# First attention: maxima in a bank of the transposed scores' ring, a step later, and values between a step's two kinds of scores

## The chip, the cores and the metric

The kernel runs on one core of one Trainium2 chip. The metric is the device time of one execution in microseconds (us). TensorE is called PE in the profile (its weight loads PEld), VectorE DVE, ScalarE ACT, GpSimd POOL, SyncE SP.

## The reference: a small latent attention, the first of four

The whole program is two attentions with a feed-forward block behind each, twice, over x of 2 x 512 x 512 in fp32: eight residual steps. The change lies in the first of them alone:

```python
C_q = x @ Wq_d + bq_d                      # 512 -> 12
C_kv = x @ Wkv_d + bkv_d                   # 512 -> 4
q = (C_q @ W_qk + b_qk).reshape(b, s, 32, 4)
scores = einsum('bqhd,bkd->bhqk', q, C_kv) / sqrt(4)
attn = softmax(scores, axis=-1)            # no mask: 512 x 512 per head
V = (C_kv @ Wv_u + bv_u).reshape(b, s, 32, 16)
out = einsum('bhqk,bkhd->bqhd', attn, V)
return out.reshape(b, s, 512) @ Wo + bo
```

There are 2 batches x 32 heads, and each head has a score matrix of 512 x 512. The keys are only four numbers wide, so the matmuls are small and the scores have to be reduced (for the maxima) and exponentiated in full.

## The kernel before

Each head's scores are computed twice. Once as they stand, queries on the partitions, only to find the maximum of each row: `score` (L586) makes one 128 x 512 block with a matmul over 32 rows of the array and reduces it on DVE (L597) to one column of `nm`. And once transposed, keys on the partitions, with the maximum already subtracted: `transposed` (L621) makes a block (L627) and ACT takes its exponential into `probs` (L630). The subtraction needs no extra operation, since the negative maxima stand in spare rows of the queries: `maxima` (L611) transposes `nm` with four matmuls (L615), adds the queries with a fifth (L616, recorded at L199), and ACT copies the result to `qm` (L618). `split` (L601), two small POOL operations, divides the maxima into a high and a low part before that. `values` (L632) multiplies four blocks of exponentials with the values; as fp32 it runs as eight matmuls of two passes.

Four heads form a quartet, one in each quarter of 32 rows of the array; matmuls in different quarters can run side by side. There are 16 quartets, u = 0 to 15 (`quartets`, L573). A quartet takes 8 steps. In each step the queue of PE receives

- `next_scores()`: two scores, of quarters 0, 1 in even steps and 2, 3 in odd ones. Scores run twelve steps ahead: those of quartet u+1 end with step 3 of quartet u, where `split` follows;
- two transposed blocks of quartet u;
- in even steps one call of `values` for a block of keys that was finished at least two steps earlier (the list `behind`);
- in odd steps a call of `slices` (L757): a piece of other work from the list `extra` (projections and head preparation of the second batch first, then division, output projection and the start of the feed-forward block); some pieces hold no matmul, and the piece `add` is a POOL operation alone. In the last quartet there are slices in every step, two in the odd ones;
- in step 6 `maxima(u + 1)`.

PE's order is that of the code here (`tc.manual_schedule(engines={PE})`), so what stands at the head of PE's queue and waits holds all that is behind it. The other engines get their instructions in an order that the framework plans.

PSUM has eight banks of 128 x 512. They are dealt out by hand (L578 to L584): scores take banks 0, 1, 2 in turn ("S"), transposed blocks 3, 4, 5 ("T"), `values` bank 6, slices bank 7. A matmul that writes a bank waits until the bank's last reader (DVE for S, ACT for T) is done. `maxima` takes its turn in the S ring. In the last quartet, when no scores are left, slices also use banks 0 to 2.

Of the kernel before, what the change touches and what calls it, by code (L numbers as in the profile page):

```python
# [38 lines left out]
B, S, D = 2, 512, 512  # L39
# [389 lines left out]
def attn_latent_small(k, a):  # L429
# [9 lines left out]
    with ExitStack() as ctx:  # L439
# [134 lines left out]
        last = len(quartets) - 1  # L574
# [7 lines left out]
        def own_bank(kind):  # L582
            turns[kind] = (turns[kind] + 1) % 3
            return k.held[:, banks[kind][turns[kind]]]  # L584
# [25 lines left out]

        def maxima(u):  # L611
            b, half, i = quartets[u]
            tp = own_bank("S")
            for qt in range(NT):
                nc.tensor.transpose(tp[:, bass.ts(qt, P)], nm[u % 2][:, qt], k.ident)  # L615
            k.correct(tp, unit, qs[b][:, 4 * half + i])  # L616
            t = lp.tile([P, S], F32R, tag="qm", name="qm")
            nc.scalar.copy(t, tp)  # L618
            qm[u] = t

        def transposed(u, kc, g):  # L621
            b, half, i = quartets[u]
            if (u, kc) not in probs:
                odd = kc % 2
                probs[u, kc] = lp.tile([P, 4, S], F32, tag="pT", name="pt") if odd else k.other()
            ps = own_bank("T")
            nc.tensor.matmul(  # L627
                ps, keys[b][rows[g], bass.ts(kc, P)], qm[u][rows[g]], start=True, stop=True
            )
            nc.scalar.activation(probs[u, kc][:, g], ps, AF.Exp)  # L630

        def values(u, kc):  # L632
            b, half, i = quartets[u]
            acc = k.held[:, of_values]
            pt = probs.pop((u, kc))
            for g in range(4):
                nc.tensor.matmul(  # L637
                    acc[rows[g]],
                    vals[b][:, kc, i],
                    pt[:, g],  # L640
                    start=(i == 0 and kc == 0),
                    stop=(i == 3 and kc == NT - 1),
                )
            if i == 3 and kc == NT - 1:
                raws[u] = one([P, S], "raw")
                nc.scalar.copy(raws[u], acc)
                extra.extend(following(u))
# [66 lines left out]
        def following(u):  # L714
            b, half, i = quartets[u]
            if half == 0:
                return [divide(u)]
            if b == 1:
                return [divide(u)] + tail() + [project(u)]
            bias = lambda: blocks[0].bias  # L720
            pairs = []
            for t in (0, 2):
                pairs += [centre(t, t + 1, bias=bias), adapt(t), adapt(t + 1), put(t), put(t + 1)]
            return (
                [divide(u), begin(), project(u)]
                + pairs
                + [keep()]
                + [product(0), product(1), centre(0, 1), product(2), product(3)]
                + [put(0, True), put(1, True), centre(2, 3)]
            )  # L730
# [8 lines left out]
        def next_scores():  # L739
            at = next(scores, None)  # L740
            if at:
                u, qt, p = at
                for g in (2 * p, 2 * p + 1):
                    score(u, qt, g)
                if (qt, p) == (NT - 1, 1):
                    split(u)

        def run(pieces):
            for piece in pieces:
                for _ in piece:  # L750
                    pass

        def fill(n, bank):
            for _ in range(n):
                nc.tensor.matmul(k.held[:, bank], unit, keys[0], start=True, stop=True)

        def slices(cost):  # L757

            if not extra:
                fill(3, k.ring[-1])  # L760
            with tc.issue_after(first):
                while extra and cost > 0:
                    done = next(extra[0], None)
                    if done is None:
                        extra.pop(0)
                    else:
                        cost -= done

        k.ring = k.EVERY
        with tc.manual_schedule(engines={mybir.EngineType.PE, mybir.EngineType.DVE}):  # L770
            k.warm(30)
            for t in range(0, NT, 2):
                pair = [k.statistics(t + i) for i in range(2)]
# [28 lines left out]
        behind = []  # L802
        with tc.manual_schedule(engines={mybir.EngineType.PE}):
            for n in range(12):
                next_scores()
                slices(1)
                fill(2, of_values)
                if n == 7:
                    with tc.issue_after(k.latest):
                        adapter_coefficients(k, a)  # L810
                if n == 8:
                    maxima(0)
            run(extra)
            extra = later
            k.ring = other
            for u in range(len(quartets)):
                if u == last:
                    k.ring = (0, 1, 2, 7)
                for step in range(8):
                    next_scores()  # L820
                    for g in (2, 3) if step % 2 == 0 else (0, 1):
                        transposed(u, step // 2, g)
                    if step == 6 and u < last:
                        maxima(u + 1)
                    if step % 2 == 0 and len(behind) > 1:
                        values(*behind.pop(0))
                        if u == last:
                            slices(1)
                    else:
                        slices(2 if u == last else 1)  # L830
                    if step % 2:
                        behind.append((u, step // 2))
            k.ring = (0, 1, 2, 3, 4, 5, 7)
            for at in behind:
                values(*at)
            run(extra)
# [4 lines left out]
def adapter_coefficients(k, a):  # L841

    nc = k.nc
    k.coef = k.const.tile([P, 1], F32, tag="coef", name="coef")
    starts = k.load_row(a["f0_starts"], 4, "f0_starts", dtype=I32)
    rows = k.load(a["c_lora"], [P, 4], "c_lora", 1)
    startf = k.sm(4, "startf", 1)
    nc.vector.tensor_copy(startf, starts)


    c = k.sm(4, "le", 1)
    nc.vector.tensor_scalar(c, startf, rows[:, 3:4], None, ALU.is_le)
    r = k.sm(3, "rank", 1)
    both = k.sm(2, "adapter", 1)
    nc.vector.tensor_tensor(both, c[:, 1:3], c[:, 2:4], ALU.mult)
    nc.vector.tensor_tensor(r[:, 0:2], c[:, 1:3], both, ALU.subtract)
    nc.vector.tensor_copy(r[:, 2:3], both[:, 1:2])
    nc.vector.tensor_tensor(r, r, rows[:, 0:3], ALU.mult)
    nc.vector.tensor_reduce(k.coef, r, AX.X, ALU.add)
# [1292 lines left out]
@with_exitstack  # L2152
def kernel(ctx: ExitStack, tc: tile.TileContext, a: dict, out: bass.AP):
    k = Block(ctx, tc, a["x"], out)
    k.hold()
    block = attn_latent_small(k, a)
    bound = CausalBound(k, a)
    attn_gqa(k, a, bound, block)
    ffn_lora(k, a, block)
    attn_mla(k, a)  # L2160
    k.release(ctx)
    with k.tc.tile_pool(name="f1", bufs=2) as own:
        experts = Experts(k, a, own)
        with k.tc.tile_pool(name="heads", bufs=1) as pool:
            rooms = HeadRooms(k, a, pool)
            experts.first(rooms.fill)
            attn_mha(k, a, bound.register(), rooms, experts)
        experts.end()
# [168 lines left out]
```

## Time and profile before

| | us |
|---|---|
| median of 3 runs | 1975.5 (1972.48 to 1975.85) |
| the profiled execution | 1973.68 |
| its span, first to last instruction | 1971.9 |
| in it: the sixteen quartets | about 42 to 254 |
| PE busy in the span | 1928.5 (98%) |
| DVE busy | 1372.9 (70%) |
| ACT busy | 932.6 (47%) |
| POOL busy | 1024.6 (52%) |
| in 233 to 254, where no scores are left: DVE busy | 6.62 of 21 |
| one reduction of scores (L597), median | 0.680 |
| one exponential (L630), median | 0.597 |

The clock of PE is full (0.998 granted). Busy shares are means over stages with different limits; what matters for this change is the order of rows between 42 and 254 us. A matmul's row is longer than the time until the next may start, because matmuls are pipelined: distances are read from start to start. Two matmuls of one line that follow each other at once are merged into one row of the timeline ("x2"). The maxima of quartets 1 to 15 are transposed at 51.91, 64.57, 76.46, 88.97, 101.08, 114.58, 126.46, 138.33, 151.04, 164.10, 180.05, 193.80, 208.34, 220.64 and 233.56 us (starts of the first L615 row of each); they mark the quartets in the timeline.

### The profile page before, as it was taken

How to read it: one execution, taken by the hardware profiler on the slowest of the kernel's cores; microseconds unless marked ns; L12 is line 12 of the kernel's file. 1: busy time of each engine (PE TensorE's matmuls, PEld its weight loads, DVE VectorE, ACT ScalarE, POOL GpSimd, SP SyncE). 2: the span in 40 equal slices, each digit the busy share in tenths (PEclk: the TensorE clock that was granted, in tenths of full speed). 3: DMA queues.
4: the chain of work that ended last, by engine and by line, in shares of the span. 5: the costliest groups of instructions: out<-in, count | busy, mean ns of one | idle time of the engine just before them, and what ended most of it. 6: DMA issues, size and time to landing. Idle time of an engine off the chain costs nothing.

```text
span 1971.9 us, 40474 instructions
## 1 busy us (share of the span) xinstructions
PE 1928.5 (98%) x15608; PEld 1193.8 (61%) x15608; DVE 1372.9 (70%) x3456; ACT 932.6 (47%) x2450; POOL 1024.6 (52%) x1122
## 2 busy tenths in 40 slices
PE   9989999999999999999999999999999999999998
PEld 5333356777777777777776545666566544654654
DVE  8889658767776676777775576777677755847843
ACT  3876624444444443544443266666666311641640
POOL 4331055776756667677764256565656445216211
PEclk9999999999999999999999999999999999999999
DMA  4010222322321322232223213020101002002001
GB/s 136 17 44 1 76 68 70 87 77 89 93 71 40 97 76 81 76 97 76 78 79 84 71 22 109 7 73 7 62 13 55 28 6 48 2 2 44 1 2 43
DMA packets 69152, 108.96 MB, mean 55 GB/s; under 512 B 13906, under 2 KB 48722, under 8 KB 61908
## 3 DMA queue, kind: packets, MB, share of 16 engines
q1 hardware_dynamic: 68660, 104.15, 18.0%
q8 instruction: 127, 2.08, 0.5%
q0 software_dynamic: 288, 2.10, 0.3%
q14 instruction: 77, 0.63, 0.1%
HBM read 80.00 MB, written 4.19 MB: 43 GB/s over the span
## 4 chain that ended last, share of the span: by engine, by line
PE 87%; DVE 5%; POOL 4%; issue 1%; ACT 1%; DMA 0%; SPq 0%; DVEq 0%; ACTq 0%; POOLq 0%
PE held L1004 13%; PE held L281 11%; PE held L1139 9%; PE held L190 8%; PE held L357 8%; PE held L637 3%; PE held L589 3%; PE held L1076 3%; PE sc L190 2%; PE held L473 2%; PE tp L190 2%; PE held L1498 2%; PE held L1495 2%; PE pj L190 1%; PE held L1496 1%
## 5 line engine op out<-in xcount | busy, mean ns | idle before, releaser
L302 ACT ACTIVATE room<-room,nmax 128x128 f32<-128x128 f32 (+3 forms) x384 | 212.6, 557 | 354.9 <-DVE nmax L292 352.4
L281 PE MATMUL held<-kT,q 128*32 128x32 f32 (+15 forms) x4096 | 264.0, 397 | 6.2 <-DVE invs L310 2.3
L292 DVE CUSTOM_DVE_ANT_0 room<-held,mask 128x128 f32<-128x128 f32 (+3 forms) x384 | 178.9, 487 | 63.7 <-PE held L281 58.2
L281 PEld LDWEIGHTS held<-kT,q 128*32 128x32 f32 x4096 | 143.5, 110 | 87.4 <-issue 35.8
L357 PE MATMUL held<-turned,vals 32*128 32x384 f32 (+7 forms) x2784 | 189.5, 416 | 1.2 <-issue 1.2
L597 DVE TENSOR_REDUCE nm<-held 128x1 f32<-128x512 f32 x256 | 161.5, 682 | 23.5 <-PE held L627 13.9
L357 PEld LDWEIGHTS held<-turned,vals 32*128 32x128 f32 (+1 forms) x2784 | 149.3, 167 | 40.1 <-issue 23.5
L315 ACT ACTIVATE room<-room,invs 128x128 f32<-128x128 f32 (+3 forms) x312 | 151.3, 551 | 41.0 <-DVE invs L310 40.9
L254 DVE TENSOR_TENSOR rows<-rows,held 128x512 f32<-128x512 f32 x198 | 129.4, 673 | 31.9 <-PE held L1004 31.4
L330 DVE STREAM_TRANSPOSE turned<-room 128x1152 f32<-128x1152 f32 x80 | 107.9, 1361 | 40.7 <-ACT room L315 21.6
L243 POOL TENSOR_TENSOR rstd<-ve,mhalf 128x1 f32<-128x1 f32 x64 | 36.2, 569 | 177.1 <-DVE ve L241 177.1
L1165 POOL TENSOR_TENSOR q<-q,room 128x256 f32<-128x256 f32 x64 | 45.2, 727 | 123.6 <-DVE q L1148 113.0
L1183 POOL TENSOR_TENSOR q<-q,cosq 128x512 f32<-128x512 f32 x60 | 88.0, 1467 | 31.5 <-DVE t L1180 31.5
L1139 PE MATMUL held<-room,w 128*128 128x256 f32 x384 | 95.0, 383 | 0.0
L1184 POOL TENSOR_TENSOR q<-q,t 128x512 f32<-128x512 f32 x64 | 86.7, 1355 | 6.3 <-DVE q L1183 2.5
L302 ACT ACTIVATE probs<-probs,nmax 128x128 f32<-128x128 f32 (+3 forms) x128 | 70.7, 553 | 40.6 <-DVE nmax L292 39.8
L589 PEld LDWEIGHTS held<-keys,qs 32*128 32x128 f32 x256 | 30.9, 181 | 94.2 <-DVE nm L597 68.1
L1004 PE MATMUL held<-w,ctxT 128*128 128x256 f32 x360 | 86.5, 383 | 0.1
L630 ACT ACTIVATE pt<-held 128x512 f32<-128x512 f32 x128 | 69.7, 599 | 30.0 <-PE held L627 25.7
L589 PE MATMUL held<-keys,qs 32*128 32x512 f32 x256 | 77.1, 494 | 5.4 <-DVE nm L597 5.1
L630 ACT ACTIVATE room<-held 128x512 f32<-128x512 f32 x128 | 69.7, 599 | 26.7 <-PE held L627 23.2
L1519 POOL TENSOR_TENSOR q<-t,t 64x512 f32<-64x512 f32 x62 | 78.9, 1272 | 4.9
(435 smaller groups left out, 4949.4 us busy)
## 6 DMA issues: line engine op xcount, KB each, us to landing
w<-in_b_wq SPq DMA_DIRECT2D x16, 1024.0 KB, 4.9
w<-in_b_wo SPq DMA_DIRECT2D x16, 1024.0 KB, 4.9
vals<-v SPq DMA_DIRECT2D x256, 64.0 KB, 2.1
w<-in_m_wo SPq DMA_DIRECT2D x8, 1024.0 KB, 6.7
w<-in_b_wk SPq DMA_DIRECT2D x16, 256.0 KB, 2.8
w<-in_b_wupv SPq DMA_DIRECT2D x16, 256.0 KB, 2.6
w<-in_m_wqn SPq DMA_DIRECT2D x8, 384.0 KB, 3.5
rows<-in_x SPq DMA_DIRECT2D x8, 256.0 KB, 4.6
```

The source lines that it names most:

```text
L190: last = self.nc.tensor.matmul(out, lhsT, rhs, start=(i == 0), stop=(i == len(pairs) - 1))
L254: self.nc.vector.tensor_tensor(x, x, ps.rearrange("p (t d) -> p t d", t=2), op)
L281: nc.tensor.matmul(ps[32 * i : 32 * i + 32, a - lo : b - lo], q[:, at : at + 32], keys[:, a:b], start=True, stop=True,)
L292: nc.vector.tensor_tensor_reduce(out=row, in0=ps[:, :kv], in1=self.mask_back[:, :kv] if qt % 2 else self.mask[:, S - kv :], op0=ALU.add, o ...
L302: nc.scalar.activation(row, row, AF.Exp, bias=nmax, scale=-1.0, accum_out=total[:, qt : qt + 1])
L315: self.nc.scalar.activation(row, row, AF.Identity, scale=each)
L357: self.nc.tensor.matmul(out[:, :, :n], values(i, j), rhs, start=(j == blocks[0]), stop=(j == stop[i]),)
L589: nc.tensor.matmul(ps, qs[b][rows[g], 4 * half + i, bass.ts(qt, P)], keys[b][rows[g]], start=True, stop=True,)
L597: k.latest = nc.vector.tensor_reduce(nm[u % 2][:, qt, at : at + 1], ps, AX.X, ALU.max, negate=True).ins
L630: nc.scalar.activation(probs[u, kc][:, g], ps, AF.Exp)
L1004: k.nc.tensor.matmul(out, lhsT[:, i, bass.ts(t, P)], rhs[i], start=not (after or t or i), stop=i == 1, skip_group_check=True,)
L1139: nc.tensor.matmul(out, lhsT[:, c], rhs[:, c], start=c == 0, stop=c == 1)
```

## The change

Three things, all in the loop over quartets and in `maxima`:

- `maxima` takes its bank from the T ring.
- `maxima(u + 1)` moves from step 6, behind the transposed blocks, to step 7, between the scores and the transposed blocks.
- In a step, `values` (or the slice) comes between the scores and the transposed blocks, and no longer behind them; only the slice of step 7, and the additional slice of the last quartet's even steps, stay behind. The pairs of quarters change places: transposed blocks take quarters 0, 1 in even steps and 2, 3 in odd ones. Step 7 of the last quartet has one slice where it had two.

```diff
         def maxima(u):
             b, half, i = quartets[u]
-            tp = own_bank("S")
+            tp = own_bank("T")
...
                 for step in range(8):
                     next_scores()
-                    for g in (2, 3) if step % 2 == 0 else (0, 1):
+                    if step == 7 and u < last:
+                        maxima(u + 1)
+                    pair = (2, 3) if step % 2 else (0, 1)
+                    held = step % 2 == 0 and len(behind) > 1
+                    if held:
+                        values(*behind.pop(0))
+                    elif step < 7:
+                        slices(2 if u == last else 1)
+                    for g in pair:
                         transposed(u, step // 2, g)
-                    if step == 6 and u < last:
-                        maxima(u + 1)
-                    if step % 2 == 0 and len(behind) > 1:
-                        values(*behind.pop(0))
-                        if u == last:
-                            slices(1)
-                    else:
-                        slices(2 if u == last else 1)
+                    if step == 7 or held and u == last:
+                        slices(1)
                     if step % 2:
                         behind.append((u, step // 2))
```

## Prediction

> **What bounds the kernel now.** I read the page first, then the list of waits between 50 and 245 us (the stretch of this attention's sixteen quartets), then the timeline there, one engine at a time. Below, S is the pair of score matmuls of a step (L589), T its pair of transposed-score matmuls (L627), V one block of values (L637), X a slice of other work, M the four transposes and the correction for the maxima (L615, L199).
>
> ```profile
> PE 1928.5 (98%) x15608; PEld 1193.8 (61%) x15608; DVE 1372.9 (70%) x3456; ACT 932.6 (47%) x2450; POOL 1024.6 (52%) x1122
> ```
>
> ```profile
> PEld held L589 <- DVE nm L597: 61.4, 90, 1.0
> ```
>
> TensorE is busy throughout, and after the attention nothing stands still for long: what this stretch gains or loses, the end gains or loses. Inside the stretch the longest wait is that of S for a reduction on DVE. Whether that wait costs anything is seen in the timeline. Columns are start, length, engine, line. First PE with a full slice (two fp32 matmuls, L473) in each odd step:
>
> ```profile
> 85.58 0.50 PE L589 MATMUL held<-keys,qs 32*128 32x512 f32 x2
> 85.58 0.49 PE L627 MATMUL held<-qm,keys 32*128 32x512 f32 x2
> 86.01 1.07 PE L637 MATMUL held<-room,vals 128*32 128x512 f32 x8
> 87.00 0.50 PE L589 MATMUL held<-keys,qs 32*128 32x512 f32 x2
> 87.01 0.50 PE L627 MATMUL held<-qm,keys 32*128 32x512 f32 x2
> 87.44 1.13 PE L473 MATMUL held<-w,wv_diag 128*128 128x512 f32 x2
> 88.50 0.50 PE L589 MATMUL held<-keys,qs 32*128 32x512 f32 x2
> ```
>
> S and T start together: they use different quarters of the array's rows, so four matmuls take one pass. From start to start a pass takes 0.43 us, V 1.00, X 1.06, so two steps take 0.43+1.00+0.43+1.06 = 2.92 us with no gap: PE sets the pace. Then PE, DVE and ACT where the slices hold no matmul:
>
> ```profile
> 124.49 0.50 PE L589 MATMUL held<-keys,qs 32*128 32x512 f32 x2
> 124.50 0.50 PE L627 MATMUL held<-qm,keys 32*128 32x512 f32 x2
> 124.86 0.50 PE L589 MATMUL held<-keys,qs 32*128 32x512 f32 x1
> 125.77 0.50 PE L589 MATMUL held<-keys,qs 32*128 32x512 f32 x1 [0.42 <-DVE nm L597]
> 125.77 0.50 PE L627 MATMUL held<-qm,keys 32*128 32x512 f32 x2
> 126.46 0.63 PE L615 MATMUL held<-ident,nm 128*128 128x128 f32 x4 [0.19 <-DVE nm L597]
> 126.84 0.48 PE L199 MATMUL held<-qs,unit 128*128 128x512 f32 x1
> 127.25 1.06 PE L637 MATMUL held<-pt,vals 128*32 128x512 f32 x8
> 128.25 0.50 PE L589 MATMUL held<-keys,qs 32*128 32x512 f32 x2
> ```
>
> ```profile
> 125.02 2.48 DVE L597 TENSOR_REDUCE nm<-held 128x1 f32<-128x512 f32 x4 [0.22 <-PE held L627]
> 128.78 1.89 DVE L597 TENSOR_REDUCE nm<-held 128x1 f32<-128x512 f32 x3 [1.27 <-PE held L627]
> ```
>
> ```profile
> 125.09 1.08 ACT L630 ACTIVATE room<-held 128x512 f32<-128x512 f32 x2 [0.37 <-PE held L627]
> ```
>
> Here a loop sets the pace: S at 124.49, its reduction starts at 125.02 and takes 0.69, the second S of the next step needs that bank and starts at 125.77 (1.28 after the first S), V comes 0.43 later and S again 1.00 after V: 1.28+0.43+1.00 = 2.71 us for two steps. M costs more than its own 0.8 us here: it takes a bank of the S ring, waits for a reduction (126.46 in place of 126.20), and DVE then idles 1.27 us, because S of step 7 stands behind M and V.
>
> **The change, part by part.** It adds and removes no instruction, transfer or element; it reorders PE's queue and gives M a bank of the T ring. SP's and POOL's queues keep their order (the two small POOL operations that split the maxima are issued at step 3 as before, now four steps ahead of M).
>
> *Values or slice between S and T.* Before the queue reads [S T] V [S T] X. After it reads S V [T S] X [T S] V: a T pair now shares its pass with the next step's S pair. The pairs (0,1) and (2,3) are swapped, so the two pairs of a pass still use four different quarters. Within a quartet the number of passes stays, so a PE-paced pair of steps stays at 2.92. In the DVE-paced stretch the second T of a step now stands in front of S and waits for the bank of the T three back: T at 124.50, exponent at 125.09, done 0.60 later, hence 1.19, and about 0.05 to hand over (125.71 to 125.77 on the DVE side): 1.24, against 1.28 for the wait of S that is there anyway. I take 2.71 as unchanged, by 0.04 us of cover; without that cover every such pair of steps is longer by what ACT is late. On ACT itself the two exponents of a step need 1.08 us; four of them and a copy of a head fit 2.71, just.
>
> *The ends of the quartet.* At step 7 the queue becomes [T6 S7] M T7 X, and at step 0 of the next quartet S0 V [T0 S1]. X now lies between T7 and S0, so each has a pass to itself: nine passes in a quartet in place of eight. A pass with a single pair takes as long as one with two, as the end of the stretch shows, where no scores are left:
>
> ```profile
> 230.22 0.50 PE L627 MATMUL held<-qm,keys 32*128 32x512 f32 x2
> 230.65 1.06 PE L637 MATMUL held<-room,vals 128*32 128x512 f32 x8
> ```
>
> So +0.43 per quartet where PE sets the pace; where it doesn't, nothing (lower end zero).
> [...] I hold to the row: the whole pass is paid.
>
> *M in the T ring.* M no longer waits for DVE (its bank's exponent was issued before V and is done), which takes away 0.25 us at about half the quartets and 0.04 elsewhere. But it takes one of three banks: T7's first matmul needs the bank of T6's first (exponent done 1.19 after T6), its second that of T6's second (0.59+1.08 = 1.67, with the hand-over 1.73). M ends at 0.43+0.81 = 1.24. So T7's second waits 0.48, and X, S0 and V stand behind it. Nothing covers that where PE sets the pace.
>
> From the pass [T6 S7] to [T0 S1] the new order therefore takes 1.73 + 0.43 (T7) + X + 0.43 (S0) + 1.00 (V) = 3.59 + X; with no matmul in X, S0 shares T7's pass: 1.73+0.43+1.00 = 3.16. The two steps before it take the larger of 2.71 and 1.86+X. Against this stands the interval in the timeline of before, from S of step 5 to S of step 1 of the next quartet. By the time of M:
> - full slices. M at 52: 2.92+4.65 = 7.57 against 6.85 (49.79 to 56.64), +0.72. At 76 (the slice before M is four transposes, hence 2.71): +0.70. At 221: 7.57-6.67 = +0.90. At 180 and 194, with slices of 1.72: 3.58+5.31 = 8.89 against 8.03 and 8.18, +0.86 and +0.71. At 164 DVE has no gap (7.32): PE alone would give +0.25, a DVE that runs dry +0.9; I take +0.6. Together +4.5.
> - short slices (a head, 0.43, or four transposes, 0.59). At 65: 2.71+4.02 against 6.58, +0.15; at 89: 2.92+4.02-6.45 = +0.49; at 138 and 208: 2.71+4.18-6.46 = +0.43 each; at 151 (DVE with two more operations): +0.3. Together +1.8.
> - no matmul in the slice. At 115: 2.92+3.16-6.47 = -0.39; at 126: 2.71+3.16-6.46 = -0.59. Together -1.0.
> - at 101 the slice waits for POOL and DVE until 104.31 either way, and S0 and V follow as before: 0.
> - the ends: S0 of the first quartet alone +0.43; in the last but one T3 alone (no scores left) +0.43, and the wait of T7 +0.48. Together +1.3.
>
> Sum: 4.5+1.8-1.0+1.3 = +6.6 us. The last quartet holds the same pieces in the same number (eleven slices, twelve before with the last one empty): 0.
> The profiled execution took 1973.68 us, 1971.9 of it span and 1.8 around it: 1980.3 for it. It lies 1.8 under the median of the three runs, 1975.5; the middle of the four times is 1974.6, and 1974.6+6.6 is 1981, which I predict.
>
> **The rivals.**
> - *DVE sets the pace and gains (ends faster).* Freed of M, the S ring lets S7 go out one V and one M earlier, and the DVE gap of 1.27 us before 128.78 shrinks. Where that decides, a boundary gains 0.6 (the case at 126). For all fifteen that is -9; it needs eight of fifteen to break even with 0.7 lost at the others. For it: DVE has a gap of 0.6 to 1.4 us behind M at thirteen of the fifteen. Against it: at all but two (those at 115 and 126) the slice of step 7 puts a matmul and a pass of its own behind T7, and the rows around 86 show PE without a gap. With ten gaining, -6+3.5 = -2.5; at twelve -5: about 1969.
> - *The T wait takes the place of the S wait (slower still).* 0.04 us of cover is thin. If exponents come 0.2 late (the head copies share ACT, which is busy 10.0 of 11 us between 65 and 76), each of some 24 DVE-paced pairs of steps loses 0.2: +5 on top, 1986; at 0.5 it is +12, 1993.
> - *Nearly nothing.* If the single passes overlap their neighbours, the sum is 6.6-5.4 = about +1: 1976.
>
> **How the numbers follow.** Forecast (+4 to +10, 1978 to 1985 of its own): 0.56. Gain: 0.13. T wait: 0.14. Nearly nothing: 0.17. Slower by over 0.2% (3.95 us, about what a measurement of this kernel can tell from no change) are the forecast and the T wait: 0.70; within 0.2%: 0.17; faster: 0.13. The range of 8 in 10 takes in the nearly-nothing case with the scatter of the runs (1972.5 was seen) and the T wait at 0.2 and a little more: 1972 to 1988.
>
> **What would show it.** In the changed profile: M directly behind a pass [T S], with no wait for DVE; T of step 7 with its second matmul some 0.5 us late, released by an exponent (L627 waiting for L630, 4.6 us in six places before, more than 10 after); S of step 0 alone in a pass of 0.43 before V; 2.92 and 2.71 us per two steps unchanged in the middle of quartets; the quartet from M at 76 to M at 89, 12.5 us, near 13.4; that from 115 to 126, 11.9, near 11.3. I am wrong if the middle of the quartets changes its period, or if the second T of step 7 finds its bank free.

## The result and the profile after

| | before | after |
|---|---|---|
| median, us | 1975.5 (1972.48 to 1976.82, 5 runs) | 1982.67 (1981.73 to 1984.58, 5 runs) |
| ratio, 95% interval | | 1.0039 (1.0027 to 1.0050) |
| the profiled execution; its span | 1973.68; 1971.9 | 1983.25; 1981.5 |
| first M of all to the start of the last matmul of V | 218.14 | 225.42 (+7.28) |

The changed kernel is 0.39% slower, 7.2 us by the medians. Nearly all of it lies in the sixteen quartets: from the first maxima (37.1 and 37.5 us) to the last values block they take 7.28 us more.

The page shows nothing of this; PE's share does not move. Columns: engine, busy us (share) x instructions.

```profile
PE 1940.8 (98%) x15608; PEld 1201.5 (61%) x15608; DVE 1372.4 (69%) x3456; ACT 931.2 (47%) x2450; POOL 1025.8 (52%) x1122
```

The instructions are as many as before, yet PE is "busy" 12.3 us longer. Rows overlap, and a matmul that has half the array to itself (S at 189.18 below, alone for 0.43 us) or stands under a lower clock (PE is busy for 3.40 of the 3.40 us from 1761.9, at a granted clock of 0.50) counts as busy all the same. So the page can't tell; the order of rows can. The waits between 50 and 250 us (engine, line, releaser: us in all, times, longest us):

```profile
PEld held L627 <- ACT room L630: 37.8, 47, 0.9
...
PEld held L627 <- ACT pt L630: 27.3, 51, 0.9
...
PEld held L589 <- DVE nm L597: 2.3, 4, 1.4
```

The 61.4 us that S waited for DVE have become 65.1 us that T waits for ACT. It was said in the prediction that T would now stand in front of S. That the sums are alike says little about time: the wait of one has taken the place of the wait of the other. What the change costs is seen where one quartet ends. PE where slices are full (start, length, engine, line):

```profile
185.38 0.49 PE L627 MATMUL held<-qm,keys 32*128 32x512 f32 x2
185.38 0.62 PE L589 MATMUL held<-keys,qs 32*128 32x512 f32 x2
185.93 0.66 PE L615 MATMUL held<-ident,nm 128*128 128x128 f32 x4
186.34 0.47 PE L199 MATMUL held<-qs,unit 128*128 128x512 f32 x1
186.75 0.79 PE L627 MATMUL held<-qm,keys 32*128 32x512 f32 x2
187.47 0.73 PE L755 MATMUL held<-keys,unit 128*128 128x512 f32 x2
188.13 1.12 PE L905 MATMUL held<-w,w 48*128 48x512 f32 x2
189.18 0.50 PE L589 MATMUL held<-keys,qs 32*128 32x512 f32 x2
189.61 1.06 PE L637 MATMUL held<-room,vals 128*32 128x512 f32 x8
```

and, on ACT, the exponentials of T6, for whose banks T7 waits:

```profile
185.91 1.09 ACT L630 ACTIVATE pt<-held 128x512 f32<-128x512 f32 x2 [0.35 <-PE held L589]
```

Here is the end of the quartet as the prediction drew it. Pass [T6 S7] at 185.38, M 0.55 behind it, T7 at 186.75 with a row of 0.79 in place of 0.49: its second matmul starts 0.30 late, and X (two rows, 187.47) starts 0.72 behind T7 in place of 0.43. S0 then has 0.43 to itself (189.18 to 189.61) before V. No gap is long, and yet the boundary is longer.

Where slices hold no matmul (the quartet whose M are at 115 and 126 in the kernel before) the end is as drawn as well, and a pair of steps in the middle reads

```profile
126.02 0.49 PE L627 MATMUL held<-qm,keys 32*128 32x512 f32 x2
126.02 0.50 PE L589 MATMUL held<-keys,qs 32*128 32x512 f32 x2
...
127.20 0.49 PE L627 MATMUL held<-qm,keys 32*128 32x512 f32 x1 [0.45 <-ACT pt L630]
127.20 0.65 PE L589 MATMUL held<-keys,qs 32*128 32x512 f32 x2
127.78 1.07 PE L637 MATMUL held<-room,vals 128*32 128x512 f32 x8
128.78 0.49 PE L627 MATMUL held<-qm,keys 32*128 32x512 f32 x2
```

with, on DVE,

```profile
126.62 2.50 DVE L597 TENSOR_REDUCE nm<-held 128x1 f32<-128x512 f32 x4 [0.28 <-PE held L589]
```

T's wait ends at 127.20, 1.18 after the first T, earlier than the 1.24 predicted. But the second row of S is 0.65 long in place of 0.50: its second matmul waits for a reduction that starts 0.60 after S (126.02 to 126.62), where it was 0.53 before. So V follows 0.58 behind the pass, and two steps take 2.76 us, not 2.71.

One thing was in no step of the prediction. First DVE, then PE in the changed kernel, around 78 us:

```profile
78.01 0.43 DVE L560 COPY wv_diag<-a_bvu 128x512 f32<-128x512 f32 x1 [1.40 <-POOL qs L482]
```

```profile
79.09 0.49 PE L589 MATMUL held<-keys,qs 32*128 32x512 f32 x1 [1.12 <-DVE nm L597]
```

DVE's order is the planner's. With PE's new order it puts a copy (L560, a bias spread out for a later slice, into a buffer that POOL still reads) in front of two reductions. The copy waits 1.40 us for POOL, the reductions with it, and S on PE 1.12 us.

Behind the attention the programs are the same in kind, and still the spans differ by 9.6 us where the quartets differ by 7.3. Windows of 3.41 us at half the granted clock account for most: by the granted clock the profile before has three of them behind the attention (at 1161.9, 1902.6, 1970.9 us), the one after four (1594.7, 1761.9, 1912.1, 1980.4). The last of each begins 1 us before the end, when PE has nothing more to do; each of the others costs, by an estimate from the clock of 0.50, about half its length, 1.7 us (within such a window in E10, below, a block V takes 1.86 us in place of 1.00, 179.45 to 181.31). How much of a run they take differs between executions of one kernel: of 24 runs of the kernel before the shortest, 1971.49 us, had a mean granted clock of 0.999, the longest, 1978.55 us, one of 0.995. So they are part of the scatter between runs. Where one falls within the quartets of a profile, its cost is taken off below, and this is said. For every run the mean granted clock is on record; what it lacks to 1, times the span, is by estimate what the half clock took (3.9 us in the profile before, at 0.998; half of its two windows of 3.41 us and of the 1 us of the third is 3.9 too), below called the lost clock: 5.2 us in the mean of the five runs after.

### The profile page after: what moved, and what is told of

Same layout as the page of the kernel before. It is cut to its first block, busy times and chain, and to the rows that moved or that the text cites. A ratio compares the mean times of both kernels' runs of the same rounds, so it can differ in the third digit from the quotient of the medians.

```text
span 1981.5 us, 40456 instructions
## 1 busy us (share of the span) xinstructions
PE 1940.8 (98%) x15608; PEld 1201.5 (61%) x15608; DVE 1372.4 (69%) x3456; ACT 931.2 (47%) x2450; POOL 1025.8 (52%) x1122
## 4 chain that ended last, share of the span: by engine, by line
PE 87%; POOL 6%; DVE 3%; ACT 2%; issue 1%; DVEq 0%; POOLq 0%; ACTq 0%
PE held L1006 13%; PE held L281 11%; PE held L1141 9%; PE held L190 8%; PE held L357 8%; PE held L637 3%; PE held L627 3%; PE held L1078 3%; PE sc L190 2%; PE held L473 2%; PE tp L190 2%; PE held L1500 2%; PE pj L190 1%; PE held L1497 1%; PE held L1498 1%
## 5 line engine op out<-in xcount | busy, mean ns | idle before, releaser
L627 PEld LDWEIGHTS held<-qm,keys 32*128 32x128 f32 x256 | 29.2, 181 | 91.2 <-ACT room L630 40.2
L1141 PEld LDWEIGHTS held<-room,w 128*128 128x128 f32 x384 | 71.4, 190 | 14.3 <-issue 2.0
L2089 POOL TENSOR_SCALAR_AFFINE_SELECT room<-room 128x512 f32<-128x512 f32 x32 | 20.4, 638 | 114.9 <-ACT room L2085 109.4
```

Source lines behind the costliest of these rows:

```text
L627: nc.tensor.matmul(ps, keys[b][rows[g], bass.ts(kc, P)], qm[u][rows[g]], start=True, stop=True)
L1141: nc.tensor.matmul(out, lhsT[:, c], rhs[:, c], start=c == 0, stop=c == 1)
```

## The experiments

The theory: at each boundary with a matmul in its slice PE runs one pass more (0.43 us), and M, now in the T ring, makes T7's second matmul wait (0.22 to 0.42). The rivals: that the wait for the T ring costs everything and the pass nothing (it would overlap its neighbours, the "nearly nothing" of the prediction), or that the price is M's place, or the planner's new DVE order.

All ten at a glance. "Quartets" is the distance from the first M to the start of the last matmul of V; in brackets after 1.7 (3.4 for the 6.8 us of E2, 43.4 to 50.2, at 0.50) is taken off for half-clock windows in it. "PE-paced" is the quartet whose M are at 180 and 194 in the kernel before, "no slices" that from 115 to 126.

| | median us (range, runs) | ratio to before (95%) | quartets | PE-paced | no slices |
|---|---|---|---|---|---|
| before | 1975.5 | 1 | 218.14 | 13.75 | 11.87 |
| after | 1982.67 | 1.0039 (1.0027 to 1.0050) | 225.42 | 14.60 | 11.38 |
| E1 after, M in the S ring | 1981.22 (1979.01 to 1984.49, 6) | 1.0035 (1.0021 to 1.0048) | 224.31 | 14.55 | 11.53 |
| E2 before, M in the T ring | 1975.23 (1973.13 to 1979.92, 12) | 1.0007 (0.9998 to 1.0016) | 221.16 (217.75) | | |
| E3 after, last slice before T7 | 1972.97 (1969.95 to 1974.76, 11) | 0.9987 (0.9978 to 0.9996) | 215.37 | 13.69 | 11.38 |
| E4 before, M between S7 and T7 | 1981.68 (1980.15 to 1983.07, 5) | 1.0037 (1.0024 to 1.0050) | 223.51 | 14.50 | 12.02 |
| E10 E4, M in the T ring | 1979.94 (1976.54 to 1982.77, 8) | 1.0033 (1.0023 to 1.0044) | 224.31 (222.6) | 14.25 | 12.01 |
| E5 after, last slice behind S0 | 1982.01 (1977.62 to 1984.55, 9) | 1.0032 (1.0020 to 1.0044) | 224.87 (223.2) | 14.18 | 11.38 |
| E6 after, copy held back | 1979.73 (1978.58 to 1983.56, 11) | 1.0024 (1.0015 to 1.0033) | 224.17 | | |
| E7 E3 and E6 | 1971.82 (1970.90 to 1976.49, 12) | 0.9985 (0.9976 to 0.9994) | 215.04 | | |
| E8 E7, scores in front of T | 1969.85 (1967.82 to 1973.11, 9) | 0.9973 (0.9962 to 0.9983) | 214.20 | 13.64 | 11.27 |
| E9 E8, own buffers | 1967.27 (1965.95 to 1969.66, 6) | 0.9967 (0.9955 to 0.9979) | 211.85 | 13.64 | 11.26 |

### E1 and E2: the bank of the maxima

E1 is the kernel after with the old bank for M; E2 is the kernel before with the new one.

```diff
E1, to after                      E2, to before
-            tp = own_bank("T")   -            tp = own_bank("S")
+            tp = own_bank("S")   +            tp = own_bank("T")
```

> The changed kernel with the maxima back in a bank of the S ring; they stay in step 7. Theory A (the change costs by two things at the end of each quartet: 0.42 us in which T7's second matmul waits for its bank, and a pass of 0.43 us for a single pair): T7 finds its bank free, 15 times 0.42 = 6 us come back, so about 1 us above the kernel before, 6 below the changed kernel. Theory B (the cost lies in the new order within the steps, T in front of S, and in what the planner makes of DVE's and ACT's queues): the ring of the maxima does nothing, 7 us above the kernel before as the changed kernel.

> The kernel before with one edit, the maxima in a bank of the T ring; still in step 6. Theory A: T7 is issued 2.2 us after T6, when all exponents are done, so no wait on the T ring; the maxima lose their wait for DVE of 0.25 us at about seven quartets: 1 to 2 us below the kernel before. Theory C (three T banks are too few wherever the maxima take one): 15 times 0.4 = 6 us above it.

Both missed. E1 was to give back the wait of T7, and gives back almost nothing: 1.0035 of before. Its end of a quartet:

```profile
185.36 0.62 PE L589 MATMUL held<-keys,qs 32*128 32x512 f32 x2
186.18 0.63 PE L615 MATMUL held<-ident,nm 128*128 128x128 f32 x4 [0.20 <-DVE ln_mv L207]
...
186.96 0.49 PE L627 MATMUL held<-qm,keys 32*128 32x512 f32 x2
187.39 0.73 PE L755 MATMUL held<-keys,unit 128*128 128x512 f32 x2
```

T7 no longer waits (a row of 0.49, X 0.43 behind it). But M does: 0.82 behind the pass where after has 0.55, since in the S ring behind S7 its bank is that of step 6's second score, whose reduction is still on. The wait has gone from T7 to M: in this quartet 14.55 in place of 14.60. So neither ring is free for M at this place, and E1 does not tell the price of T7's wait.

E2 was to gain 1 to 2 us and gained nothing. In the old place M lost 0.14 us of its wait (T to M 0.55 in place of 0.69), not the 0.25 put down for it, and from the second quartet on none takes over 0.1 us more. The T ring in itself is harmless; it costs only where M stands directly in front of T7.

### E3: the last slice back in front of T7

E3 leaves T7 and S0 in one pass and gives T7's bank the time of a slice.

```diff
                     if held:
                         values(*behind.pop(0))
-                    elif step < 7:
+                    else:
                         slices(2 if u == last else 1)
...
-                    if step == 7 or held and u == last:
+                    if held and u == last:
                         slices(1)
```

> The changed kernel with the slice of step 7 in front of T7, as in the other odd steps (behind the maxima). T7 then shares its pass with S0 and its bank comes free while the slice runs. Theory A: 3.73 us in place of 4.64 from pass T6 S7 to pass T0 S1 where PE sets the pace, the same gain with a short slice, none where the slice has no matmul: about 12 times 0.85 = 10 us below the changed kernel, 3 below the kernel before. Theory B: as the changed kernel, 7 us above the kernel before, since the order within the steps stays.

Right in size: 9.7 us under the median of after, 1.8 under that of before in the same runs (1974.81), with the whole interval of the ratio under 1. Its end of a quartet:

```profile
180.46 0.66 PE L615 MATMUL held<-ident,nm 128*128 128x128 f32 x4
...
181.19 0.63 PE L755 MATMUL held<-keys,unit 128*128 128x512 f32 x2
...
182.80 0.50 PE L627 MATMUL held<-qm,keys 32*128 32x512 f32 x2
182.80 0.49 PE L589 MATMUL held<-keys,qs 32*128 32x512 f32 x2
183.23 1.07 PE L637 MATMUL held<-room,vals 128*32 128x512 f32 x8
```

T7 and S0 start together at 182.80, T7 has its normal length, V is 0.43 behind. The quartet is back from 14.60 to 13.69 and the one without slices keeps its gain (11.38). So, with the rest of the change in place, the whole loss lies in where the slice of step 7 stands; that rest, taken together, gains a little (E3 is 0.9987 of before). This alone does not tell the pass from the wait.

### E4 and E10: M at its new place in the order of before

E4 moves M alone, E10 moves it and gives it the T ring; S, T, V and X keep their old places. Now S7 has a pass to itself (M stands between it and T7).

```diff
                     next_scores()
+                    if step == 7 and u < last:
+                        maxima(u + 1)
                     for g in (2, 3) if step % 2 == 0 else (0, 1):
                         transposed(u, step // 2, g)
-                    if step == 6 and u < last:
-                        maxima(u + 1)
```

> The kernel before with one edit, the maxima moved from behind T6 to between S7 and T7 (still in the S ring; S before T, values and slices behind them as before). This parts the pass S7 T7 and makes nothing else of the change. Theory A: one pass of 0.43 us more where PE sets the pace (about ten quartets), no wait for a T bank, nothing or a few tenths gained where DVE does: about 4 us above the kernel before. Theory B: nothing, within 1 us of the kernel before.

> The version with the maxima between S7 and T7 in the old order, but with their bank in the T ring. There T6 lies a block of values before S7, so every exponent is done and neither the maxima nor T7 should wait for a bank: only the parted pass is left. Theory A: 0.43 us at the quartets where PE sets the pace, about ten, 3 to 4 us above the kernel before; in the profile the maxima start 0.43 us behind S7 (0.7 to 0.85 with the S ring, where they waited for the reduction of step 6). If the single pass were free: level with the kernel before or a little below.

E4 costs 1.0037, more than expected, and the reason is the one of E1. PE at the same place of a quartet, E4 and then E10:

```profile
184.10 0.52 PE L589 MATMUL held<-keys,qs 32*128 32x512 f32 x2
184.82 0.63 PE L615 MATMUL held<-ident,nm 128*128 128x128 f32 x4 [0.19 <-DVE nm L597]
```

```profile
185.56 0.51 PE L589 MATMUL held<-keys,qs 32*128 32x512 f32 x2
185.99 0.66 PE L615 MATMUL held<-ident,nm 128*128 128x128 f32 x4
...
186.81 0.49 PE L627 MATMUL held<-qm,keys 32*128 32x512 f32 x2
187.23 0.73 PE L755 MATMUL held<-keys,unit 128*128 128x512 f32 x2
```

In the S ring M starts 0.72 behind the single pass of S7, in the T ring 0.43: no wait at all, and here T7 does not wait either (row 0.49, X 0.42 behind), since T6 went out a V earlier. So E10 is one single pass and nothing else: S7 takes 185.56 to 185.99, 0.43 us, with half of the array's quarters unused. The quartet takes 14.25 in place of 13.75, +0.50, and the quartets together +4.5 (222.6 against 218.14); +3 to +4 was expected. In one quartet (M at 78.92) 0.4 us of this is a slice that waits for the copy of L560. The single pass is paid in full, and the 0.07 beyond it in the quartet shown are not accounted for.

### E5: the pass shared, T7's wait kept

In E5 the last slice goes behind S0 of the next quartet, so that [T7 S0] share a pass, directly behind M as in the kernel after.

```diff
                     next_scores()
+                    if step == 0 and u > 0:
+                        slices(1)
...
-                    if step == 7 or held and u == last:
+                    if (step == 7 or held) and u == last:
                         slices(1)
```

> The changed kernel with the slice of step 7 moved to step 0 of the next quartet, behind its scores: T7 shares its pass with S0, but the maxima stand directly in front of T7 as before. So the single pass goes and T7's wait of 0.42 us stays. Theory A: 0.43 us less at the eleven or twelve quartets whose slice holds a matmul, 5 us below the changed kernel, 2 above the kernel before. If the wait alone were the cost: no gain, as the changed kernel. If the pass alone were: level with the version that puts the slice before T7.

By its time a miss: 1.0032, no better than after within the intervals. By its profile the mechanism is there:

```profile
185.87 0.66 PE L615 MATMUL held<-ident,nm 128*128 128x128 f32 x4
...
186.68 0.78 PE L627 MATMUL held<-qm,keys 32*128 32x512 f32 x2
186.97 0.50 PE L589 MATMUL held<-keys,qs 32*128 32x512 f32 x2
187.41 0.73 PE L755 MATMUL held<-keys,unit 128*128 128x512 f32 x2
...
189.12 1.06 PE L637 MATMUL held<-room,vals 128*32 128x512 f32 x8
```

T7's second matmul still waits 0.29 (186.97 behind 186.68), but S0 goes with it, and V comes 3.25 behind M; in the kernel after it is 3.68 (185.93 to 189.61). The quartet takes 14.18 in place of 14.60, 0.42 less; seven quartets each gain 0.40 to 0.45. With E3 this splits the loss of 0.91 between after and E3 in this quartet:

- after to E5, 0.42: the single pass;
- E5 to E3, 0.49: T7's wait of 0.29, and about 0.2 that X gains directly behind M. M takes 0.73 to X in E3 (180.46 to 181.19) and 0.81 to T7 in E5 (185.87 to 186.68); X takes 1.61 behind M (181.19 to 182.80) and 1.71 behind T7 (187.41 to 189.12).

What the time of E5 loses again lies mostly at one place, shortly ahead of 109:

```profile
108.22 0.49 PE L589 MATMUL held<-keys,qs 32*128 32x512 f32 x1 [0.88 <-DVE nm L597]
108.64 1.86 PE L473 MATMUL held<-w,wv_diag 128*128 128x512 f32 x2
```

S0's second matmul waits 0.88 us for a reduction that stands on DVE behind another of the planner's operations (L542, which itself waits 1.38 us for POOL), and a half-clock window follows at 108.9 (granted clock 0.50 from there to 112.3; the slice of 1.06 us takes 1.86). The quartet takes 15.68 where after has 13.48. That is 2.2 of the 3 us that the seven shared passes gain. The window belongs to this one execution, but the runs' clocks tell why the median is as high: the lost clock is 7.0 us in the mean of E5's nine runs against 5.2 in that of after's. With it taken off each run, E5 is 3.2 us under after and 5.1 over before, which is what its quartets say (223.2 against 225.42 and 218.14) within 1 us. The 5 us that were to come back did not all come. Where the windows fall in the other runs isn't shown.

### E6 and E7: the copy that the planner put in front

E6 is the kernel after with the copy of L560 issued only behind the reductions that stand ahead of it in the code; E7 is E3 with the same.

```diff
             bv_rep = one([P, KC, P], "wv_diag")
-            nc.vector.tensor_copy(bv_rep, ...)
+            with tc.issue_after(k.latest):
+                nc.vector.tensor_copy(bv_rep, ...)
```

> The changed kernel with one dependency more: the DVE copy for the bias (L560) is issued behind the reductions traced before it. In the changed kernel it stands in front of two reductions, waits 1.4 us for POOL there, and PE stalls 1.1 us near 78 us. Theory: that stall is the planner's queue order and no part of the change's own order: 1.4 us less, 5.5 above the kernel before; the stretch around 76 to 85 us loses its 1.1 us wait for a reduction. Rival: the copy stands there because nothing else can: another wait takes its place, no gain.

> The changed kernel with the slice of step 7 in front of T7 and the bias copy held back, both. Expected: the gains add, 1.8 plus 1.4 us below the kernel before: 3.2 below it.

E6 right: the quartet of the stall goes from 13.93 to 12.49, 1.44 less, and the next one gives back 0.20. (By the medians it is 2.9 under after, of which 1.4 are lost clock, 5.2 us in the mean after against 3.8 here.) So 1.2 of after's 7.3 us come from the planner's order on DVE, not from PE's. E7 is 1.2 under E3 by the medians, but the intervals overlap, and in its profile the gain is passed on: the stalled quartet goes from 12.95 to 11.51, the next from 12.51 to 13.61, since the slice that uses the copy now waits for it. The sum that was expected, 3.2 below before, came (3.0 by the ratio), but the gains did not add as it said: the quartets gain 0.33. In E8, the next version, that is to be seen at the slice itself:

```profile
78.51 1.13 PE L473 MATMUL held<-w,wv_diag 128*128 128x512 f32 x2 [0.81 <-DVE wv_diag L561]
```

### E8: scores first in the pass

E8 lets scores run one step further ahead and issues them directly in front of T, so that S is the first of the four in a pass, with the order of everything else as in E7.

```diff
             k.ring = other
+            next_scores()
             for u in range(len(quartets)):
...
                 for step in range(8):
-                    next_scores()
...
                         slices(2 if u == last else 1)
+                    next_scores()
                     for g in pair:
                         transposed(u, step // 2, g)
```

> As the version with the slice before T7 and the copy held back, but with the scores one step further ahead and in front of T in each shared pass (S T in place of T S); all else in the same order. In the changed kernel a pair of steps paced by DVE takes 2.76 us in place of 2.71, and the reduction of the first score starts 0.59 us after its matmul in place of 0.53. Theory: the pair that stands first in a pass is delivered 0.06 us earlier, so S first gives 2.71 again: some 24 pairs, 1.3 us less than with T first, 4.5 below the kernel before. Rival: the 0.06 comes from somewhere else (the wait of T for ACT): 2.76 stays.

Right, 1969.85 us. Lines are shifted by one here (S is L590, T L628, V L638). PE and DVE in a stretch without slices:

```profile
121.04 0.50 PE L590 MATMUL held<-keys,qs 32*128 32x512 f32 x2
121.05 0.50 PE L628 MATMUL held<-qm,keys 32*128 32x512 f32 x2
...
122.32 0.50 PE L590 MATMUL held<-keys,qs 32*128 32x512 f32 x1 [0.41 <-DVE nm L598]
122.32 0.50 PE L628 MATMUL held<-qm,keys 32*128 32x512 f32 x2
122.76 1.06 PE L638 MATMUL held<-room,vals 128*32 128x512 f32 x8
123.75 0.49 PE L590 MATMUL held<-keys,qs 32*128 32x512 f32 x2
```

```profile
121.58 2.48 DVE L598 TENSOR_REDUCE nm<-held 128x1 f32<-128x512 f32 x4 [0.22 <-PE held L628]
```

The reduction starts 0.54 after S in place of 0.60, V follows 0.44 behind the pass in place of 0.58, and two steps take 2.71 again (121.04 to 123.75). So the reader that is awaited longest is best served by the first pair of the pass: here that is worth 0.05 us for two steps.

### E9: own buffers

E9 takes away what makes the copy wait: the copy's tile and that of the product of L542 shared a buffer (`wv_diag`) with the tile that POOL reads for the heads; each gets its own, and the copy need not be held back.

```diff
-            wv_diag = one([P, KC, H, 4], "wv_diag")
+            wv_diag = one([P, KC, H, 4], "wv_fold")
...
-            bv_rep = one([P, KC, P], "wv_diag")
-            with tc.issue_after(k.latest):
-                nc.vector.tensor_copy(bv_rep, ...)
+            bv_rep = one([P, KC, P], "bv_rep")
+            nc.vector.tensor_copy(bv_rep, ...)
```

> The version with the scores first in each pass, but in place of the dependency that held the bias copy back (L560), that copy and the DVE product of the output fold (L542) each get a buffer of their own, so neither waits until POOL has read the heads' buffer. In the version before this, the slices behind those two wait about 1.0 us near 77.5 and 1.2 us near 103. Theory: the waits are for the shared buffer; both go, 2 us less, 7 us below the kernel before. Rival: the two DVE operations stand behind reductions in DVE's queue anyway, and the slices wait as long: no gain, 5 below the kernel before.

Right: 1967.27 us, 0.9967 of before (0.9955 to 0.9979) and 15.4 under after: the fastest of all. Its PE at the place where E8 waited 0.81:

```profile
77.38 0.47 PE L199 MATMUL held<-qs,unit 128*128 128x512 f32 x1
77.69 1.02 PE L473 MATMUL held<-w,bv_rep 128*128 128x512 f32 x2
```

The slice follows M at once, 0.31 behind the correction. Both waits are gone: the two quartets in which they stood take 12.43 and 12.26 us in place of 13.53 and 13.48, and all quartets 211.85 us, 6.3 less than before.

## Why the prediction was right, point by point

The time was right (1981.0 against 1982.67; +6.6 against +7.2), and the likeliest case is the one that came. The terms by the same views, from the pass of step 5 to that of step 1 around each M:

| M at (in before) | before | predicted | measured |
|---|---|---|---|
| 52 | 6.85 | 7.57 | 7.75 |
| 65 | 6.58 | 6.73 | 6.82 |
| 76 | 6.66 | 7.36 | 8.79 |
| 89 | 6.45 | 6.94 | 6.87 |
| 101 | 7.67 | 7.67 | 7.70 |
| 115 | 6.47 | 6.08 | 6.01 |
| 126 | 6.46 | 5.87 | 5.87 |
| 138 | 6.46 | 6.89 | 6.88 |
| 151 | 6.79 | 7.09 | 7.20 |
| 164 | 7.32 | 7.92 | 7.86 |
| 180 | 8.03 | 8.89 | 8.82 |
| 194 | 8.18 | 8.89 | 9.04 |
| 208 | 6.46 | 6.89 | 6.86 |
| 221 | 6.67 | 7.57 | 7.49 |

- **The single pass, +0.43 where PE sets the pace.** Right, and shown twice by taking it apart: sharing it again gives 0.42 (E5), adding one alone costs 0.50 in the same quartet (E10). The row that the prediction held to bears it out: a pass with two of its four quarters in use takes as long as a full one, and so it did here (0.43 in E10, 185.56 to 185.99, and 0.43 in E3, 182.80 to 183.23).
- **T7's wait, 0.48.** There at every boundary, but 0.22 to 0.42 long. The term that was mis-sized is the 0.59 from T to its exponential: T stands first in the pass now, and the exponential starts 0.53 after it (185.38 to 185.91). So T7's second matmul starts 1.66 to 1.68 behind the pass, not 1.73; where M is late itself, up to 0.64 behind the pass, less of that is left as a wait. It was never taken away alone (E1 moves it to M, E3 takes the pass with it), so its own share of the loss is only worked out, E5 to E3.
- **M without a wait for DVE.** Half right. M stands 0.43 to 0.47 behind the pass, or 0.51 to 0.64 where S7's second matmul itself is late. But the 0.25 that the T ring was to take off M is 0.14 by E2, and E1 and E4 show a larger thing that the prediction didn't see: at the new place M *needs* the T ring, since in the S ring it waits about 0.3 us more at six of the boundaries.
- **2.92 where PE sets the pace.** Right. **2.71 where DVE does:** wrong by 0.05, for another reason than the rival's. The 0.04 of cover for T held (its wait is 1.18, not 1.24). What failed is that S, now behind T in the pass, hands its bank to DVE 0.06 later. E8 shows it by turning the order around. By the prediction's own sign ("I am wrong if the middle of the quartets changes its period") this is a miss, if a small one.
- **The case at 76, +0.70.** Wrong: +2.13. The 1.4 between are nearly all the planner's copy on DVE: with it held back (E6) the same interval takes 7.49. The text said that SP's and POOL's queues keep their order and said nothing of DVE's, which is planned anew for each order of PE; this is the step that was left out.
- **The ends, +1.3.** Wrong, about +0.4 was measured. The "S0 of the first quartet alone" was counted twice: fifteen additional passes are the fourteen boundaries and T3. And the last quartet isn't neutral: slices of two steps now stand together, and three take 2.77 us together where they took 1.05 and 1.92, which gains 0.2 in two or three places.
- **The middles of the quartets, 0.** In sum right (7.28 less the intervals' 6.9 and the ends' 0.4 leaves nothing), but made up of parts that weren't: longer by 0.12 for each pair of steps where heads are copied, by 0.06 where DVE sets the pace, and shorter by 0.29 between 143 and 149 and by 0.59 between 169 and 177 us of the kernel before. In the second of these DVE takes its operations in another order than before, in the first it doesn't. The cause of the two gains wasn't tried.

So the fourteen intervals give +6.9 where +5.3 was put down; without the 1.3 of the copy in them they give +5.6, and each is then within 0.2 us of its number. The 0.9 too much at the ends hid most of the 1.6 too little in the intervals: the mechanism was right, and that these two misses cancel is luck. The rivals: the case at 126 gained 0.59 as the first rival said, but with the one at 115 stayed alone; exponentials were not late; the passes did not overlap their neighbours.

The medians of E4, E5 and E10 lie 1.5 to 2.4 us above what their quartets account for. The lost clock closes this: it is 6.7, 7.0 and 5.9 us in the means of their runs, against 5.4, 5.8 and 3.5 in the runs of the kernel before that were taken with them. With it taken off each run, the three lie 5.2, 5.1 and 4.0 us above before in the mean, where the quartets say 5.4, 5.1 and 4.5. The same holds within 0.6 us for E1, E2 and E7 to E9.

Open: for E3, E6 and the kernel after 0.8 to 1.0 us are left between the two ways of counting. The clock of a run is on record to three digits, 2 us of its span, so it tells means and not single runs; and why some versions lost more clock than others isn't shown.

## What to carry to other kernels

Where matmuls of different quarters share the array, count passes, not instructions: here an operation put between two halves of a pair cost a whole pass where the array sets the pace (0.42 by E5, 0.50 by E10), and moving a slice by one place undid it (the quartet from 14.60 to 13.69 in E3). A ring of three banks with one more user can hand a wait on to whoever comes three turns later instead of losing it (0.30 for T7 in the kernel after, and none with the slice in between, in E3); put work of a slice's length between them. Change PE's order and the planned engines get another order too: look there for a new instruction at the head of a queue that waits for something slow (here a copy that waited 1.40 us for POOL), and take away what it waits for rather than holding it back.

## What the runs showed of the hardware

- The place in a pass matters: of four matmuls that start together, the pair issued first releases its reader mostly 0.53 to 0.54 us after its start, the second 0.56 to 0.60, mostly 0.59 (DVE's reductions and ACT's exponentials in the kernels before, after and E8).
- A slice directly behind M saves about 0.2 us against one behind a pass of T: M takes 0.73 to X in E3 and 0.81 to T7 in E5, and X 1.61 behind M and 1.71 behind T7. The cause isn't shown by these runs.
- The half-clock windows with work behind them are 3.41 us long in the profiles before and after (1161.9 and 1902.6; 1594.7, 1761.9 and 1912.1), at a granted clock of 0.50, and some come while TensorE is busy. The two stretches of E10 before and in one of them (stretch, its length, busy us (x instructions) of PE, PEld, DVE, ACT, POOL, granted PE clock, DMA share, GB/s):

```profile
176.10:179.50 3.40, 3.09 (x20) 1.17 (x20) 3.40 (x8) 1.29 (x3) 1.70 (x3) 0.99 0.01 2
179.50:182.90 3.40, 3.40 (x18) 0.94 (x14) 2.32 (x5) 1.77 (x4) 0.00 (x0) 0.51 0.02 5
```

PE was busy 3.09 of 3.40 us in the stretch before, with 0.31 us in a wait for DVE, and the clock fell from 0.99 to 0.51. In the kernel after PE was busy for 3.40 of the 3.40 us ahead of the window at 1761.9, and for 1.12 of 3.40 ahead of that at 1594.7. What decides isn't shown by these runs.
